# Three PSUM banks for side work: handed out by name from a list of free ones, in place of strictly in turn

## The chip, the cores and the metric

The kernel runs on one core of a Trainium2 chip. The metric is the device time of one execution in microseconds (us), lower is better. The engines are TensorE (PE; its weight loads are a row of their own, PEld), VectorE (DVE), ScalarE (ACT), GpSimd (POOL) and SyncE (SP, which here only issues DMAs).

## The reference, cut to what matters

Sixteen sequences of 512 tokens and 256 channels go through two layers, each followed by a residual sum and a layer norm. All arithmetic is in float32.

```python
# layer 1: a state-space layer, run forward and backward in time, 512 inner channels, 16 states
xf = silu(causal_conv(x @ in_proj_w.T)); xb = silu(causal_conv(xf))
delta, B, C = split(x_dbl); delta = softplus(delta @ dt_proj_w.T + b)
xs = cumsum(dB_u * dA_cum, 1) / (dA_cum + 1e-12)          # per channel and state
y  = einsum('bldn,bln->bld', xs, C) + u * D; y = y * silu(res)
# layer 2: a soft mixture of 16 experts with 64 slots each
logits = x2 @ se; dispatch = softmax over tokens; combine = softmax over slots
slots = dispatch.T @ x2; eout = (gelu(slots @ Wg + bg) * (slots @ Wu + bu)) @ Wd + bd
out = combine @ eout
```

## The kernel before, in words

**The scan.** For each sequence b (16 of them, called batches here) there are four parts, (direction r, pair of 128-channel chunks p) in the order (0,0), (1,0), (0,1), (1,1). A part goes over the 16 states two at a time and, inside, over its two chunks, so a part has 16 steps and a batch has 64. A step has a fixed chain over the engines: POOL multiplies `db` (L427), ACT makes the decay `h` and the factor `th` (L444, L446), DVE scans and multiplies (`h` L450 or L452, `hg` L455), POOL multiplies `hg` by `cs` (L456), and PE adds `hg` into an accumulator by transposing it (`acc`, L371), two steps later (`add_up(2)`). The buffers are three `db`, four `hg`, three `th`, three `h` in PSUM and two accumulators in PSUM.

**Diagonal states.** For two of the sixteen states (`DIAG`, 5 and 13) the product `db` is not made on POOL but on PE, as four matmuls with a diagonal matrix into a PSUM bank (`hd`, L405, function `by_diagonal`). Such a bank is taken one step before the step that scans it, at steps 3, 4, 11 and 12 of a part, and is held until the scanning step has been written out, the next step. DVE then scans in that bank.

**Side work.** All else is written as Python generators that are stepped while the scan is written out, and so are woven into its instruction order: `prep` (projections, convolution and step sizes of the next part: `pin`, `px`, `pz`, `pdu`, `pres`, `pb`), `front` (the end of layer 1 and the dispatch for the previous batch: `pyt`, `po`, `px2`, `pl`, `pd`, `pq`) and `back` (experts for two batches, and the combination: `pg`, `pu`, `peo`, `cl`, `ctp`, `cpo`). `back` gets a group of two batches every second batch, so odd batches hold the experts and even ones most of the combination. A generator yields how many PSUM banks its next piece needs; after it has written a product into a bank it yields `HOLD`, and the instructions that read the bank are written out one step later (`take_up`). In each step `beside_scan` first takes up what is held and then offers each of the three sides one piece, `front` and `back` at a pace (`paced_piece`: a credit, never above 2). `front.drain()` writes out at the end of a batch what is left of `front`.

**The banks.** Of PSUM's eight banks the scan has five; side work and the diagonal products share three (`m_ps`). They are used strictly in turn: a counter of products taken, `count`, stands for the ring. A side may go on only if the ring would not come round to a bank that is still held:

```python
oldest = min([x.hold for x in sides if x.hold is not None] + diags[:1], default=count[0])
if count[0] - oldest + self.need > BANKS:
    break
```

After the scan (the tail: end of layer 1 for the last batch, its experts and combinations) the five others are added, and the ring has eight.

The instructions of each engine stay in the order in which they are written out, except for those that the framework's scheduler is free to move; the framework puts a wait in front of the first matmul of a product until the bank's last reader has finished.

Of the kernel before, what the change touches and what calls it, by code (L numbers as in the profile page):

```python
# [9 lines left out]
F32 = mybir.dt.float32  # L10
# [4 lines left out]
PSUM = bass.MemoryType.PSUM  # L15
DRAM = bass.MemoryType.DRAM

P = 128
# [21 lines left out]
HOLD, WAIT, GAP = -1, -2, 8  # L40
# [15 lines left out]
def seq_layers(tc, ident, neghalf, a, out):  # L56
# [22 lines left out]
    with ExitStack() as ctx:  # L79
# [11 lines left out]
        scan_room = ctx.enter_context(ExitStack())  # L91
        p4 = scan_room.enter_context(tc.tile_pool(name="m_scan", bufs=3))
        dram = ctx.enter_context(tc.tile_pool(name="m_dram", bufs=3, space=DRAM))
        ps = ctx.enter_context(tc.tile_pool(name="m_ps", bufs=3, space=PSUM))
        scan_psum = ctx.enter_context(ExitStack())
        ps_acc = scan_psum.enter_context(tc.tile_pool(name="m_acc", bufs=2, space=PSUM))
        ps_h = scan_psum.enter_context(tc.tile_pool(name="m_h", bufs=3, space=PSUM))
# [1 line left out]

        BANKS = 3
        AHEAD = 8
        tail, wide = [], []
        count = [0]

        def bank(name):
            count[0] += 1
            if tail and count[0] % 8 >= 3:
                return tail[0].tile([P, 512], F32, tag="tps", name=name)  # L110
            return ps.tile([P, 512], F32, tag="mps", name=name)

        def load_x(b):
            xt = p1.tile([P, NL, DM], F32, tag="x", name=f"x_{b}")
# [12 lines left out]
        def late(ins):  # L127

            return tc.keep_in_program_order(ins)
# [258 lines left out]
        def evict():  # L388
            while evictions:
                evictions.pop(0)()  # L390

        def scan_part(b, r, p, v, accs, done, then):

            prep.drain()
            prep.gens += [[1, g] for g in [turn_pair(b, r, p, v)] + then]
            w = side[r]
            made = {}

            def by_diagonal(n, c):

                diags.append(count[0])
                made[n, c] = h = bank(f"hd_{b}_{r}_{n}_{c}")
                for lc in range(NL):
                    s = slice(lc * P, (lc + 1) * P)
                    ins = nc.tensor.matmul(h[:, s], v[c][3][:, s], dg[:, s], start=True, stop=True)  # L405
                    if lc == 0:
                        late(ins)

            chunks = (2 * p, 2 * p + 1)
            for n in range(0, NS, 2):  # L410
                q = f"{b}_{r}_{p}_{n}"
                k = 1 if n + 1 in DIAG else 2

                bs = p4.tile([P, 2, L], F32, tag="bs", name=f"bs_{q}")
                cs = p4.tile([P, 2, L], F32, tag="cs", name=f"cs_{q}")
                nc.sync.dma_start(bs[:, :k, :], v["bc"][0, n : n + k, :].unsqueeze(0).to_broadcast([P, k, L]))
                nc.sync.dma_start(cs, v["bc"][1, n : n + 2, :].unsqueeze(0).to_broadcast([P, 2, L]))
                if n + 3 in DIAG:
                    dg = p4.tile([P, L], F32, tag="dg", name=f"dg_{q}", bufs=1)
                    nc.sync.dma_start(  # L420
                        dg.rearrange("p (l s) -> p l s", l=NL),
                        diag_dram[r, DIAG.index(n + 3), :, : P * P].rearrange("l (p s) -> p l s", p=P),
                    )
                for c in chunks:
                    dt, rr, du = v[c][:3]
                    db = p4.tile([P, 2, L], F32, tag="db", name=f"db_{q}_{c}")
                    nc.gpsimd.tensor_tensor(  # L427
                        db[:, :k, :], du.unsqueeze(1).to_broadcast([P, k, L]), bs[:, :k, :], ALU.mult
                    )
                    hg = p4.tile([P, 2, L], F32, tag="hg", name=f"hg_{q}_{c}", bufs=4)  # L430
                    hs = {}
                    for j in range(2):
                        if j < k:
                            dec = h = ps_h.tile([P, L], F32, tag="h", name=f"h_{q}_{c}_{j}")
                            hs[j] = (h, dec, db[:, j, :])
                        else:
                            h = made.pop((n + j, c))
                            dec = p4.tile([P, L], F32, tag="dec", name=f"dec_{q}_{c}", bufs=2)
                            hs[j] = (h, dec, h)

                    ths = {}
                    for j in range(2) if k == 2 else (1, 0):
                        s = slice(n + j, n + j + 1)
                        nc.scalar.activation(hs[j][1], dt, AF.Exp, scale=w["A"][:, c, s])  # L444
                        ths[j] = p4.tile([P, L], F32, tag="th", name=f"th_{q}_{c}_{j}")
                        nc.scalar.activation(ths[j], rr, AF.Tanh, bias=LN_1E12 / 2, scale=w["Ah"][:, c, s])  # L446
                    for j in range(2):
                        (h, dec, add), th = hs[j], ths[j]
                        if r == 0:
                            nc.vector.tensor_tensor_scan(h, dec, add, 0.0, ALU.mult, ALU.add)  # L450
                        else:
                            nc.vector.tensor_tensor_scan(  # L452
                                h[:, ::-1], dec[:, ::-1], add[:, ::-1], 0.0, ALU.mult, ALU.add
                            )
                        nc.vector.scalar_tensor_tensor(hg[:, j, :], th, 1.0, h, ALU.add, ALU.mult)  # L455
                    nc.gpsimd.tensor_tensor(hg, hg, cs, ALU.mult)  # L456
                    pending.append(
                        (r == n == 0, n == 0, r == 1 and n == NS - 2, c, hg, accs, w, v["u"], f"acc_{q}_{c}", done)
                    )
                    evict()  # L460

                    nxt_n = n if c == chunks[0] else n + 2
                    if nxt_n + 1 in DIAG:
                        for x in sides:
                            x.take_up()
                        by_diagonal(nxt_n + 1, chunks[1] if c == chunks[0] else chunks[0])
                    beside_scan()
                    if k == 1:
                        diags.pop(0)
                    add_up(2)  # L470

        class Side:


            def __init__(self):
                self.gens, self.hold, self.need, self.left, self.credit = [], None, 0, 0, 0.0
                self.wait = self.took = self.gap = False

            def add(self, steps, gen):
                self.gens.append([steps, gen])  # L480
# [3 lines left out]

            def go(self):

                at = count[0]
                mark = next(self.gens[0][1], None)
                self.wait = mark == WAIT
                if mark == HOLD:  # L490
                    self.hold = at if self.hold is None else self.hold
                    return
                self.hold, self.gap, self.need = None, False, 0
                if mark is None:
                    self.gens.pop(0)
                elif not self.wait:
                    self.gap, self.need = mark >= GAP, mark % GAP

            def take_up(self):
                self.took = self.hold is not None or self.wait  # L500
                if self.took:
                    self.go()

            def piece(self, gaps=True):

                done = False
                while self.gens and self.hold is None and not self.wait:
                    if self.gap and self.took and gaps:
                        break
                    oldest = min([x.hold for x in sides if x.hold is not None] + diags[:1], default=count[0])  # L510
                    if count[0] - oldest + self.need > BANKS:
                        break
                    done = True
                    head = self.gens[0]
                    head[0] = max(head[0] - 1, 1)
                    fresh = len(head) == 2
                    if fresh:
                        head.append(True)
                    self.go()
                    if not fresh and (not self.gens or self.gens[0] is head):  # L520
                        break
                return done
# [14 lines left out]
        diags = []  # L537
# [3 lines left out]
        def beside_scan():  # L541
            for x in sides:
                x.take_up()
            prep.piece()
            for x in (front, back) if front.credit > back.credit else (back, front):
                x.paced_piece(gaps=not hurry)
# [478 lines left out]
        add_up(0)  # L1025
        evict()
        scan_psum.close()
        tail.append(ctx.enter_context(tc.tile_pool(name="t_ps", bufs=5, space=PSUM)))
        scan_room.close()
        wide.append(ctx.enter_context(tc.tile_pool(name="t_sb", bufs=1)))  # L1030
        BANKS = 8

        def side_by_side():
            while front.gens or back.gens:
# [61 lines left out]
```

## Time and profile before

| | us |
|---|---|
| median of 3 runs (5407.39 to 5412.11) | 5410.29 |
| the profiled execution, its time | 5411.23 |
| its span, first to last instruction | 5409.4 |
| busiest engine over the span, POOL | 4732.1 |
| start of the first batch's scan to the end of the last one's | 48.8 to 5132.3 |
| one even batch in the middle, and one odd one | 308.3 and 326.6 |
| the last batch | 369.8 |
| the tail after the scan | 277.1 |

An engine's busy time is what its own rows sum to; a wait is idle time of the waiting engine, put down to what ended it last. Batch limits are the ends of POOL's `hg` of a batch's last step. PE's times are modelled and its matmuls overlap, so PE is read by its waits more than by its share. The mean granted clock of TensorE was 0.889.

### The profile page before, as it was taken

Reading aid. Unit: us, or ns where it says so; the run is one execution under the profiler, and the core shown is the slowest. Engines: PE = TensorE matmul, PEld = TensorE weight load, DVE = VectorE, ACT = ScalarE, POOL = GpSimd, SP = SyncE. Lnnn points to the kernel's source line nnn. Section 1 sums busy time; section 2 is a strip of 40 time slices with the busy share of each in tenths; the row PEclk is TensorE's granted clock in tenths of the full one; section 3 lists DMA queues with packets and bytes.
Section 4 is the critical chain, followed back from the end, with each engine's and each line's share of the span. In section 5 each row is a group of like instructions: output and inputs, shape, how many; then the busy total and the mean of one; then the engine's idle time right before and its main releaser. Section 6 shows DMA issues by size and latency. Waiting matters only on the chain. (4 is left out here: it accounts for less than half of the span.)

```text
span 5409.4 us, 73721 instructions
## 1 busy us (share of the span) xinstructions
PE 4331.1 (80%) x24144; PEld 3390.0 (63%) x24145; DVE 4559.7 (84%) x6276; ACT 4087.2 (76%) x6515; POOL 4732.1 (87%) x2537
## 2 busy tenths in 40 slices
PE   5656666898888978788888977889787897888889
PEld 3445555676666666677656765667656776667657
DVE  7888988889898899888998888988899889988722
ACT  6677777787888778887877887788788887877641
POOL 6999999999999899998999989998999989988600
PEclk7778778898899988899888989899889998989999
DMA  4334333575446644566446754467444764457436
GB/s 137 131 117 137 125 129 131 189 230 159 156 142 212 225 149 148 158 223 213 131 144 194 232 170 153 132 212 232 149 149 146 225 224 134 145 179 234 126 103 188
DMA packets 595236, 907.73 MB, mean 168 GB/s; under 512 B 78082, under 2 KB 384898, under 8 KB 594852
## 3 DMA queue, kind: packets, MB, share of 16 engines
q1 hardware_dynamic: 521156, 859.87, 49.5%
q10 hardware_dynamic: 73696, 43.14, 2.8%
q8 instruction: 192, 3.15, 0.2%
q14 instruction: 192, 1.57, 0.1%
HBM read 840.86 MB, written 62.01 MB: 167 GB/s over the span
## 5 line engine op out<-in xcount | busy, mean ns | idle before, releaser
L456 POOL TENSOR_TENSOR hg<-hg,cs 128x1024 f32<-128x1024 f32 x1024 | 2420.8, 2368 | 128.1 <-DVE hg L455 110.0
L427 POOL TENSOR_TENSOR db<-du,bs 128x1024 f32<-128x1024 f32 (+1 forms) x1024 | 2144.4, 2098 | 232.3 <-DVE h L450 84.7
L371 PE MATMUL acc<-ident,hg 128*128 128x128 f32 x8192 | 1179.3, 295 | 203.3 <-POOL hg L456 181.6
L455 DVE SCALAR_TENSOR_TENSOR hg<-th,h 128x512 f32<-128x512 f32 x1792 | 1185.8, 678 | 177.2 <-PE acc L371 90.4
L371 PEld LDWEIGHTS acc<-ident,hg 128*128 128x128 f32 x8192 | 1044.9, 154 | 390.8 <-POOL hg L456 240.9
L452 DVE TENSOR_TENSOR_SCAN h<-h,db 128x512 f32<-128x512 f32 x896 | 1072.8, 1218 | 112.2 <-ACT h L444 107.5
L450 DVE TENSOR_TENSOR_SCAN h<-h,db 128x512 f32<-128x512 f32 x896 | 1071.1, 1217 | 48.8 <-ACT h L444 45.7
L446 ACT ACTIVATE th<-rr,Ah_f 128x512 f32<-128x512 f32 x1024 | 725.0, 714 | 186.3 <-DVE hg L455 183.1
L446 ACT ACTIVATE th<-rr,Ah_b 128x512 f32<-128x512 f32 x1024 | 721.5, 712 | 155.2 <-DVE hg L455 147.7
L444 ACT ACTIVATE h<-dt,A_f 128x512 f32<-128x512 f32 x896 | 608.2, 680 | 117.5 <-DVE hg L455 112.6
L444 ACT ACTIVATE h<-dt,A_b 128x512 f32<-128x512 f32 x896 | 608.6, 681 | 108.8 <-DVE hg L455 105.1
L687 PE MATMUL pl<-x2T,seT 128*128 128x512 f32 x512 | 299.1, 715 | 78.7 <-DVE hg L455 37.4
L405 PE MATMUL hd<-dg,duT 128*128 128x128 f32 x2048 | 305.6, 298 | 32.7 <-ACT yt L627 13.5
L830 PEld LDWEIGHTS pg<-st,Wg 128*128 128x128 f32 x2048 | 244.8, 196 | 106.2 <-issue 85.0
L405 PEld LDWEIGHTS hd<-dg,duT 128*128 128x128 f32 x2048 | 283.1, 214 | 38.4 <-ACT yt L627 15.7
L806 PE MATMUL peo<-Wd,ht 128*128 128x256 f32 x1024 | 257.0, 407 | 55.6 <-DVE rr L337 38.6
L779 PE MATMUL pu<-st,Wu 128*128 128x128 f32 x2048 | 254.5, 283 | 50.1 <-DMA Wu<-in_Wu_dram 32.7
L962 PE MATMUL cpo<-ceo,ct 128*128 128x256 f32 x1024 | 254.8, 407 | 46.9 <-DVE rr L337 39.9
L779 PEld LDWEIGHTS pu<-st,Wu 128*128 128x128 f32 x2048 | 244.9, 198 | 61.5 <-DVE h L452 24.2
L830 PE MATMUL pg<-st,Wg 128*128 128x128 f32 x2048 | 269.9, 286 | 4.1 <-DMA Wg<-in_Wg_dram 3.1
L884 PE MATMUL cl<-seT,cx 128*128 128x512 f32 x512 | 244.7, 617 | 32.5 <-DVE res L272 12.3
L806 PEld LDWEIGHTS peo<-Wd,ht 128*128 128x128 f32 x1024 | 205.3, 206 | 97.7 <-DVE rr L337 41.2
(154 smaller groups left out, 6654.8 us busy)
## 6 DMA issues: line engine op xcount, KB each, us to landing
cs<-bc SPq DMA_DIRECT2D x512, 512.0 KB, 3.9
bs<-bc SPq DMA_DIRECT2D x384, 512.0 KB, 5.1
Wg<-in_Wg_dram SPq DMA_DIRECT2D x128, 512.0 KB, 6.0
Wu<-in_Wu_dram SPq DMA_DIRECT2D x128, 512.0 KB, 6.0
Wd<-in_Wd_dram SPq DMA_DIRECT2D x128, 512.0 KB, 5.5
dg<-diag_dram SPq DMA_DIRECT2D x128, 256.0 KB, 4.2
bs<-bc SPq DMA_DIRECT2D x128, 256.0 KB, 3.6
x<-in_x_dram SPq DMA_DIRECT2D x32, 512.0 KB, 6.3
```

The source lines that it names most:

```text
L371: ins = nc.tensor.matmul(accs[c][:, s], hc[:, j, s], ident, is_transpose=True, start=False, stop=(last and j == 1 and lc == NL - 1),)
L405: ins = nc.tensor.matmul(h[:, s], v[c][3][:, s], dg[:, s], start=True, stop=True)
L427: nc.gpsimd.tensor_tensor(db[:, :k, :], du.unsqueeze(1).to_broadcast([P, k, L]), bs[:, :k, :], ALU.mult)
L444: nc.scalar.activation(hs[j][1], dt, AF.Exp, scale=w["A"][:, c, s])
L446: nc.scalar.activation(ths[j], rr, AF.Tanh, bias=LN_1E12 / 2, scale=w["Ah"][:, c, s])
L450: nc.vector.tensor_tensor_scan(h, dec, add, 0.0, ALU.mult, ALU.add)
L452: nc.vector.tensor_tensor_scan(h[:, ::-1], dec[:, ::-1], add[:, ::-1], 0.0, ALU.mult, ALU.add)
L455: nc.vector.scalar_tensor_tensor(hg[:, j, :], th, 1.0, h, ALU.add, ALU.mult)
L456: nc.gpsimd.tensor_tensor(hg, hg, cs, ALU.mult)
L779: nc.tensor.matmul(pu[:, fc * P : (fc + 1) * P], got["Wu", e][:, k, fc * P : (fc + 1) * P], st[:, k, :, j * SL : (j + 1) * SL], start=(k = ...
L806: nc.tensor.matmul(po[:, j * DM : (j + 1) * DM], ht[:, fc, :], got["Wd", e0 + j][:, fc, :], start=(fc == 0), stop=(fc == NF - 1),)
L830: nc.tensor.matmul(pg[:, fc * P : (fc + 1) * P], got["Wg", e][:, k, fc * P : (fc + 1) * P], st[:, k, :, j * SL : (j + 1) * SL], start=Fals ...
```

## The change

Banks now have names: each of the three is a pool tag of its own with one buffer, `mps0` to `mps2`. A list `free` holds the banks that nobody holds, in the order in which they were given back. `bank()` takes the first of the list and notes it in `taken`; a side keeps its own in `held` and gives them back when the instructions that read them have been written out; a diagonal product keeps its one in `diags` until its scanning step is over. A side may go on if as many banks are free as its next piece needs. Where a diagonal product is to be made and no bank is free, the one of the diagonal product just scanned is taken. In the tail the list has eight banks.

```diff
-        ps = ctx.enter_context(tc.tile_pool(name="m_ps", bufs=3, space=PSUM))
+        ps = ctx.enter_context(tc.tile_pool(name="m_ps", bufs=1, space=PSUM))
...
-        BANKS = 3
...
-        count = [0]
+        free, taken = [0, 1, 2], []
         def bank(name):
-            count[0] += 1
-            if tail and count[0] % 8 >= 3:
-                return tail[0].tile([P, 512], F32, tag="tps", name=name)
-            return ps.tile([P, 512], F32, tag="mps", name=name)
+            i = free.pop(0)
+            taken.append(i)
+            pool = ps if i < 3 else tail[0]
+            return pool.tile([P, 512], F32, tag=f"mps{i}", name=name, bufs=1)
...
-                diags.append(count[0])
                 made[n, c] = h = bank(f"hd_{b}_{r}_{n}_{c}")
+                diags.append(taken.pop())
...
+                    own = [diags.pop(0)] if k == 1 else []
                     if nxt_n + 1 in DIAG:
                         for x in sides:
                             x.take_up()
+                        if not free:
+                            free.append(own.pop())
                         by_diagonal(nxt_n + 1, chunks[1] if c == chunks[0] else chunks[0])
                     beside_scan()
-                    if k == 1:
-                        diags.pop(0)
+                    free.extend(own)
                     add_up(2)
...
             def go(self):
-                at = count[0]
                 mark = next(self.gens[0][1], None)
-                self.wait = mark == WAIT
-                if mark == HOLD:
-                    self.hold = at if self.hold is None else self.hold
+                self.held += taken
+                taken.clear()
+                self.hold, self.wait = mark == HOLD, mark == WAIT
+                if self.hold:
                     return
-                self.hold, self.gap, self.need = None, False, 0
+                free.extend(self.held)
+                self.held, self.gap, self.need = [], False, 0
...
-                    oldest = min([x.hold for x in sides if x.hold is not None] + diags[:1], default=count[0])
-                    if count[0] - oldest + self.need > BANKS:
+                    if self.need > len(free):
                         break
...
-        tail.append(ctx.enter_context(tc.tile_pool(name="t_ps", bufs=5, space=PSUM)))
+        tail.append(ctx.enter_context(tc.tile_pool(name="t_ps", bufs=1, space=PSUM)))
...
-        BANKS = 8
+        free.extend(range(3, 8))
```

More of the change, by code (lines that the diff above doesn't have):

```diff
@@ L475, in __init__ @@
             def __init__(self):
-                self.gens, self.hold, self.need, self.left, self.credit = [], None, 0, 0, 0.0
-                self.wait = self.took = self.gap = False
+                self.gens, self.held, self.need, self.left, self.credit = [], [], 0, 0, 0.0
+                self.hold = self.wait = self.took = self.gap = False
             def add(self, steps, gen):
@@ L499, in take_up @@
             def take_up(self):
-                self.took = self.hold is not None or self.wait
+                self.took = self.hold or self.wait
                 if self.took:
@@ L506, in piece @@
                 done = False
-                while self.gens and self.hold is None and not self.wait:
+                while self.gens and not self.hold and not self.wait:
                     if self.gap and self.took and gaps:
                         break
-                    oldest = min([x.hold for x in sides if x.hold is not None] + diags[:1], default=count[0])
-                    if count[0] - oldest + self.need > BANKS:
+                    if self.need > len(free):
                         break
```

## The prediction, made before the changed kernel was run

> **What bounds the kernel now.** I read the shares of the page first, then busy times by batch, then POOL's waits, then what stands behind them. In the page, look at POOL's share and at its row of the slices.
>
> ```profile
> PE 4331.1 (80%) x24144; PEld 3390.0 (63%) x24145; DVE 4559.7 (84%) x6276; ACT 4087.2 (76%) x6515; POOL 4732.1 (87%) x2537
> ...
> POOL 6999999999999899998999989998999989988600
> ```
>
> POOL is at nine tenths or more until the scan is over. The stage table says how near to its limit each batch is: an even batch, an odd one, the last, and the tail.
>
> ```profile
> core 0: us, PE busy (x) PEld busy (x) DVE busy (x) ACT busy (x) POOL busy (x), PEclk, DMA share, GB/s
> 1911.80:2220.10 308.30, 244.40 (x1274) 185.14 (x1272) 282.27 (x385) 247.85 (x414) 295.22 (x158) 0.87 0.44 140
> 2220.10:2546.70 326.60, 283.57 (x1747) 230.77 (x1746) 284.01 (x397) 261.99 (x399) 295.28 (x157) 0.94 0.66 214
> ...
> 4762.50:5132.30 369.80, 313.56 (x1835) 251.42 (x1834) 284.74 (x416) 265.33 (x416) 288.00 (x152) 0.92 0.58 188
> 5132.30:5409.40 277.10, 248.38 (x1248) 184.74 (x1246) 67.52 (x191) 77.30 (x153) 14.68 (x44) 0.97 0.46 142
> ```
>
> POOL is busy for 295 us in both kinds of batch, and the change gives it nothing less to do. So a scan batch can lose only what POOL sits idle: 13 us of an even batch, 31 of an odd one, 82 of the last. The tail is bound by PE, 248 of 277 us. POOL's waits inside the scan name DVE first:
>
> ```profile
> POOL hg L456 <- DVE hg L455: 110.0, 57, 6.3
> POOL db L427 <- DVE h L450: 84.7, 52, 6.6
> ...
> POOL db L427 <- DVE h L452: 57.2, 34, 6.3
> ```
>
> All of POOL's waits there sum to 358 us. One step further back, DVE waits for PE where a banked product or an accumulator is late:
>
> ```profile
> DVE hg L455 <- PE acc L371: 90.4, 82, 4.8
> DVE hd L452 <- PE hd L405: 76.4, 50, 8.0
> ```
>
> With `hd` on L450 (30.0) that is 197 us. And PE itself waits for banks. These four rows are waits for the last reader of a bank's former product: `rr` (L337) reads `pz`, and `hg` on L455 reads a diagonal bank.
>
> ```profile
> PE cpo L962 <- DVE rr L337: 39.9, 10, 6.4
> PE peo L806 <- DVE rr L337: 38.6, 12, 6.6
> PE pl L687 <- DVE hg L455: 37.4, 12, 5.0
> ...
> PE px L668 <- DVE hg L455: 31.7, 6, 6.1
> ```
>
> Following each product's bank to its last reader, such waits come to 579 us of PE, 345 of them at the four steps of a part in which a diagonal bank is taken (steps 3, 4, 11 and 12: 60 + 78 + 71 + 135). The timeline shows one reach POOL, at the ninth step of an even batch:
>
> ```profile
> 1959.93 1.98 PE L405 MATMUL hd<-dg,duT 128*128 128x128 f32 x8 [2.25 <-ACT yt L627]
> ...
> 1962.01 1.23 DVE L450 TENSOR_TENSOR_SCAN hd<-dec,hd 128x512 f32<-128x512 f32 x1 [2.48 <-PE hd L405]
> ...
> 1966.42 2.35 POOL L427 TENSOR_TENSOR db<-du,bs 128x1024 f32<-128x1024 f32 x1 [1.51 <-issue]
> ```
>
> The diagonal product waited 2.25 us for a bank that ACT was to copy out, DVE's scan 2.48 us for the product, and POOL lost 1.51 us. But most do not arrive: even batches have 48 us of PE bank waits each and 13 us of idle POOL, odd ones 34 and 31.
>
> **What the Trainium skill says.** "PSUM — Partial Sum Buffer", section "Engine vs sequencer instructions": matmuls start and complete in program order. The trace agrees: where `pd` waited 3.31 us for a diagonal bank at 2485.92 us, the accumulation behind it began only after it. The same page's summary tells to guard PSUM by bank; here every product does wait for its bank's last reader. "Perfetto Trace Analysis", section "Optimization Strategy": a gap that repeats on the engine that should be full can mean too little PSUM for the next tile. The gaps do repeat (`px` six times, once per even batch), though on PE and not on POOL. "ScalarE: Activation LUTs", section "What ACT_TABLE_LOAD costs", gives 1283 ns for a load; the trace has 1283 ns.
>
> **The change part by part.** Matmuls, reads, DMAs and POOL's instructions are the same in number; only places and banks change.
>
> *Side work moves forward.* In the order written out, `cl`, `ctp`, `cpo` stand 5.5, 5.0 and 4.8 steps earlier on average, `pg`, `pu`, `peo` 3.1, `pl` 1.2, `pd` 1.5; `hd` and `pdu` stay. Twelve pieces that `front.drain()` wrote at batch ends (one `pq` in each of twelve batches) go into the scan. POOL's idle time there is near zero at the last three steps, so this is worth nothing by itself; the scan's next steps are its cover, and without it 12 x 3.5 us = 42 us would be at stake.
>
> *What moves along.* A piece's DMAs go with it on SP: an expert's `Wg`, `Wu`, `Wd` (0.4 us to issue, 6.0, 6.0, 5.5 to landing) pass some `bs` and `cs` loads. These are asked for up to three buffers ahead, about 15 us at 5 us a step against 5.1 and 3.9 to landing, and that hides it; with the cover gone, POOL's 69 us of `db` waits with no releaser shown ("issue") would be where it shows, by 0.4 us for each load passed, at most 19 us for an odd batch's 48. On POOL the layer norms' small operations move too (four of 0.2 to 1.0 us per norm), same count, 0.
>
> *Between batches.* Moving forward takes work out of even batches and into odd ones. Pricing each product by its PE time in the chain (32 `pu` or 8 `cl` records 3.5 us, others by their columns), that is 7.8 us of PE from each even batch to an odd one. From the table, 39 us more PE goes with 18 us more POOL idle, 0.47 per us, so +3.7 us in six odd batches and as much less in six even: 0.
>
> *Tail.* One `cl` pair fewer is left over: 8 records of the 3.45 us that the chain shows for such a group, on the engine that sets the tail: -3.5 us.
>
> *Table loads.* ACT has 334 loads for 337; the last batch has 25 for 32. 7 x 1.283 = 9 us of ACT there, in the batch with 82 us of idle POOL. ACT waits for DVE and DVE for ACT in turn (`h` L452 for ACT `h` 107.5 us), so I let half through: -4.5 us.
>
> *Banks.* For each product I set how many steps its bank's last reader stands ahead of the last accumulator step before it. With DVE as reader, four steps ahead cost 2.2 us on average before and three steps 0.97; 54 and 285 products become 40 and 332. With ACT, four steps cost 0.62, and 296 become 342. All distances weighted so, PE's waits before products go from 806 to 818 us: no gain in the sum. They change place, though. Products that waited for a diagonal bank (about 104 us: the `pl`, `px` rows and `pd` 18.6, `pyt` 8.5, `cl` 7.5) mostly no longer do: the distance of four before such a bank occurs three times in two batches before and once after. The waits that take their place fall on other products, and odd batches lose the pair that stood straight before idle POOL (`pd` on the diagonal bank 3.3 us, then POOL 5.1; `pl` on `pz` 3.1, then POOL 2.6). Passed on at the whole kernel's ratio, 358 us of POOL wait to 806 of PE wait, 0.44, two thirds of 104 us are -31 us; the waits that come instead (+12 net over all, so +81 in places) I charge at 0.2, because they are shorter (means of 0.6 to 1.0 us, that the three `db` and four `hg` buffers hold off): +16 us. Bounds: nothing replaces them, -46 us at full rate; all pass at 0.44, +5 us.
>
> *Free-list test in place of the ring.* No instruction. A product that goes ahead where the ring had held it brings its reader into ACT or DVE one step later, ahead of the scan's own `th` or `hg` queued there; ACT's excess over POOL in stretches of four steps grows from 115 to 145 us (loads of each engine between scan steps, row means). At 0 to 1, 0 to +30 us; I take 0, since DVE's falls by 22.
>
> Sum: -3.5 - 4.5 - 31 + 16 = -23 us on the profiled execution's 5411.2 (0.9 above the median): 5388.
>
> **The rivals.** *A, the waits only move.* The weighted sum says so outright (806 to 818), and the even batches show PE waits that cost POOL nothing. Then only the tail's 3.5 us is left: 5407. Against it: two of an odd batch's largest POOL gaps follow bank waits that go. *B, slower: the diagonal product queues behind `pz`.* A pair of `pz` banks is given back with `rr` only just written into DVE's queue, and `by_diagonal` comes right behind. Diagonal products on a `pz` bank whose reader was written out at most one step earlier go from 17 to 47. `cpo` and `peo` waited up to 6.4 and 6.6 us in that seat. A late diagonal product stops DVE's scan, which nothing passes; 30 more at the sample's 1.51 us of POOL idle are +45 us, 5455. For it: the scan depends on `hd` directly and on `cpo` only through PE's order. Against it: most such readers stand two steps ahead, a distance that cost `hd` 0.2 us on average. It decides once PE's waits in front of `hd`, 33 us now, pass some 80. *C, it doesn't free the ring.* Where two sides hold two and one bank, nothing is free either way and the order stays; the moved positions above exclude that.
>
> **How the numbers follow.** A measurement of this kernel tells about 0.2%, 11 us, from no change. Faster as summed 0.50, A 0.20, B and other harmful places 0.30. The same pattern repeats in six pairs of batches, so 5 us per pair is already 30: the faster case's own range is 5335 to 5398. The range to B's end is 5335 to 5455, with one in ten outside on each side.
>
> **What would show it.** Right: POOL waits in the scan below 340 us, odd batches at 322 or less, even ones at 308 or less, tail about 274, `pl` and `px` no longer waiting for `hg` L455. A: the same waits under other names, batches within 1 us. B: DVE `hd` waiting for PE `hd` well over 106 us, odd batches above 330. Wrong altogether: POOL's busy time per batch changed, or a tail longer by more than 5 us.

## The result, and the profile after

The change makes the kernel slower: 5461.65 us median (5445.26 to 5467.65) against 5408.84 us for the kernel before on the same chip, ratio 1.0092, interval 1.0069 to 1.0116. The prediction was 5388 us with a range to 5455 us, so both the sign and the range missed. The profiled execution took 5445.26 us, the shortest of its runs; what is taken apart below is its 34 us over the profiled one of before. Where the 16 us up to the median lie, no trace shows.

The page of the changed kernel, shares and POOL's row of the 40 slices:

```profile
PE 4326.4 (79%) x24131; PEld 3376.8 (62%) x24145; DVE 4561.5 (84%) x6276; ACT 4082.7 (75%) x6512; POOL 4737.9 (87%) x2537
...
POOL 6999999998999899998999989999899989987810
```

No engine has noticeably more to do than before (POOL 4737.9 us for 4732.1); POOL's row only goes on one slice longer. The stage table of the changed kernel, for an even batch, an odd one, the last, and the tail:

```profile
core 0: us, PE busy (x) PEld busy (x) DVE busy (x) ACT busy (x) POOL busy (x), PEclk, DMA share, GB/s
1935.20:2245.50 310.30, 240.87 (x1291) 180.97 (x1290) 282.91 (x384) 248.78 (x414) 295.26 (x157) 0.92 0.44 137
2245.50:2580.10 334.60, 288.61 (x1725) 232.49 (x1727) 283.77 (x398) 262.41 (x402) 295.83 (x157) 0.92 0.66 211
4824.50:5194.30 369.80, 309.03 (x1818) 248.61 (x1820) 282.49 (x413) 254.32 (x407) 288.11 (x151) 0.93 0.59 184
5194.30:5443.10 248.80, 236.14 (x1230) 176.90 (x1229) 66.84 (x190) 76.98 (x153) 14.79 (x45) 1.00 0.50 158
```

Two things happened. The scan ends at 5194.3 us instead of 5132.3, 62 us later, with POOL as busy per batch as before: the odd batch shown has 39 us of idle POOL for 31, the even one 15 for 13. And the tail is 28 us shorter, 248.8 for 277.1. The sum is the 34 us.

POOL's waits inside the changed kernel's scan (us in total, times, longest):

```profile
POOL db L427 <- issue: 114.8, 59, 3.6
POOL hg L456 <- DVE hg L455: 84.9, 64, 6.8
POOL db L427 <- DVE h L452: 84.6, 41, 6.1
POOL db L427 <- DVE h L450: 77.8, 67, 3.5
```

The same first row in before's view:

```profile
POOL db L427 <- issue: 69.2, 33, 3.2
```

All rows summed alike over each kernel's scan, POOL waits 422 us, before 366. The row that grew most is `db` "issue", 69 to 115 us; `db` behind DVE's `h` on L452 grew by 27 and `hg` fell by 25. "Issue" isn't a late load here: the `bs` loads are asked for over 20 us ahead and land after some 4 us, and all 59 of these waits end 0.13 us behind one of DVE's scans, which gives a `db` buffer back. Behind them stand DVE's own waits, same stretch:

```profile
DVE h L452 <- ACT h L444: 126.4, 82, 6.8
DVE hg L455 <- PE acc L371: 113.6, 81, 6.8
DVE hd L452 <- PE hd L405: 78.4, 42, 7.5
DVE h L450 <- ACT h L444: 57.3, 71, 5.9
...
DVE hd L450 <- PE hd L405: 19.9, 22, 4.5
```

Before's rows for ACT's decays, which the prediction did not show:

```profile
DVE h L452 <- ACT h L444: 107.5, 94, 6.2
...
DVE h L450 <- ACT h L444: 45.7, 33, 3.4
```

This is the reading that the prediction lacked: it followed DVE's waits back to PE alone. All rows in which DVE waits for ACT sum to 295 us, before 240; all in which it waits for PE to 300 us, before 314. So the added waits of DVE are booked to ACT, not to late banks. (A wait is booked to what ended it last; the third set of experiments comes back to this.) PE's own waits for the last reader of a bank, counted alike over both whole traces, are 643 us after and 642 before. They did change place; three of the new rows of PE:

```profile
PE pres L212 <- DVE res L272: 50.9, 9, 8.4
PE hd L405 <- DVE rr L337: 46.3, 16, 5.4
...
PE px L670 <- DVE res L272: 36.4, 6, 8.0
```

Most of the tail's gain, 20 of the 28 us, lies in one place, the dispatch of the last batch. The first table is of before, the second of the changed kernel; the second row of each is that stretch:

```profile
5132.30:5177.00 44.70, 40.70 (x190) 30.54 (x189) 12.60 (x35) 14.06 (x31) 3.28 (x8) 0.98 0.39 127
5177.00:5248.00 71.00, 57.97 (x202) 34.04 (x200) 16.20 (x42) 31.59 (x67) 1.70 (x4) 0.93 0.14 45
```

```profile
5194.30:5234.50 40.20, 37.07 (x178) 27.19 (x178) 12.50 (x34) 14.06 (x31) 3.33 (x9) 1.00 0.41 136
5234.50:5285.60 51.10, 50.52 (x204) 31.16 (x203) 15.01 (x41) 31.25 (x67) 1.70 (x4) 1.00 0.20 66
```

71.0 us became 51.1 for the same products, and PE, idle for 13 us there before, is busy throughout. PE's waits in that stretch, before and after:

```profile
PE pd L704 <- ACT et L700: 10.2, 4, 3.5
```

```profile
PE pd L706 <- ACT et L702: 0.6, 1, 0.6
```

These are not waits for banks. `pd` waits for its own input `et`, which ACT makes from `pl`. In before's trace PE takes `pd` straight behind `pl` four times, in the changed kernel's twice, since parts of `cl` and of the next `pl` stand between.

### The profile page after: what moved, and what is told of

Read it like the earlier page. It is cut to its first block, busy times and chain, and to the rows that moved or that the text cites. A ratio compares the mean times of both kernels' runs of the same rounds, so it can differ in the third digit from the quotient of the medians.

```text
span 5443.1 us, 73707 instructions
## 1 busy us (share of the span) xinstructions
PE 4326.4 (79%) x24131; PEld 3376.8 (62%) x24145; DVE 4561.5 (84%) x6276; ACT 4082.7 (75%) x6512; POOL 4737.9 (87%) x2537
## 5 line engine op out<-in xcount | busy, mean ns | idle before, releaser
L452 DVE TENSOR_TENSOR_SCAN h<-h,db 128x512 f32<-128x512 f32 x896 | 1077.3, 1222 | 130.7 <-ACT h L444 126.4
L444 ACT ACTIVATE h<-dt,A_f 128x512 f32<-128x512 f32 x896 | 611.1, 683 | 134.7 <-DVE hg L455 130.5
L444 ACT ACTIVATE h<-dt,A_b 128x512 f32<-128x512 f32 x896 | 608.7, 681 | 123.8 <-DVE hg L455 122.5
L405 PE MATMUL hd<-dg,duT 128*128 128x128 f32 x2048 | 315.0, 303 | 104.9 <-DVE rr L337 46.3
L689 PE MATMUL pl<-x2T,seT 128*128 128x512 f32 x512 | 286.5, 685 | 86.1 <-ACT cm L900 19.3
L964 PE MATMUL cpo<-ceo,ct 128*128 128x256 f32 x1024 | 237.4, 386 | 31.9 <-DVE rr L337 14.1
L721 PE MATMUL pq<-dis,xn 128*128 128x256 f32 x1024 | 244.8, 393 | 15.2 <-ACT cm L900 15.2
```

The lines of the kernel that those rows point to most:

```text
L452: nc.vector.tensor_tensor_scan(h[:, ::-1], dec[:, ::-1], add[:, ::-1], 0.0, ALU.mult, ALU.add)
```

## The experiments

One point of the text ahead is wrong. It says that before's three banks are used strictly in turn. Its `count` assumes that; but a tag with three buffers hands out whichever buffer the framework finds free as it places the instructions, and in the program as built only about 45 in 100 products take the next bank in turn. So the change has three parts, not two: the **test** (ring or free list), the **choice of bank in the scan** (the framework's, or the list's by name), and the choice **in the tail**. The table collects every kernel by these parts; "held" and "diagonals" mean the ring test against these banks alone. Times are us; the ratio is to before on the same chip and comes from all executions of a kernel, while a scan end and a tail are read from its one profiled execution. Executions of one kernel lie up to 30 us apart (e11; after 22, e1 16), so a difference of 10 or 20 us between two scan ends is read together with the medians.

| kernel | test | choice in scan / tail | scan end | tail | ratio, interval |
|---|---|---|---|---|---|
| before | ring | framework / framework | 5132.3 | 277.1 | 1 |
| e4 | ring | framework / framework | 5132.7 | 281.8 | 0.9997, 0.9989 to 1.0005 |
| e5 | ring | framework / names | 5132.4 | 257.5 | 0.9964, 0.9952 to 0.9976 |
| e1 | ring | names / names | 5158.4 | 250.4 | 0.9983, 0.9977 to 0.9990 |
| e2 | ring | names in turn / same | 5263.2 | 252.2 | 1.0169, 1.0151 to 1.0187 |
| after | free list | names / names | 5194.3 | 248.8 | 1.0092, 1.0069 to 1.0116 |
| e3 | free list | framework / framework | 5214.2 | 274.6 | 1.0133, 1.0119 to 1.0148 |
| e6 | ring: diagonals | names / names | 5180.2 | 251.2 | 1.0042, 1.0029 to 1.0055 |
| e7 | ring: held | names / names | 5275.8 | 251.8 | 1.0207, 1.0193 to 1.0221 |
| e17 | ring: `prep` only | names / names | 5227.6 | 246.5 | 1.0126, 1.0108 to 1.0145 |
| e18 | ring: `prep` only | framework / names | 5182.9 | 250.7 | 1.0068, 1.0048 to 1.0089 |

In the diffs below, lines that only keep the old count are left out.

**First set: the parts one by one.** e1 keeps the changed kernel's names and lets the old test decide, so that side work is written out exactly as before:

```diff
-                    if self.need > len(free):
+                    oldest = min([x.at for x in sides if x.at is not None] + marks[:1], default=count[0])
+                    if count[0] - oldest + self.need > BANKS:
```

> Side work stands at exactly the steps of the kernel before (its ring test decides when a side may go on); only the bank of each product comes from the list of free names, as in the changed kernel. Theory N (fixing a bank by name at the time of writing costs, because the pool no longer gives a product whichever buffer comes free): slower than before by 25 us or more, 5435 to 5465, tail near 277. Theory G (side work going ahead past held banks is what costs): as before, 5400 to 5415.

e2 is before with its banks named strictly in turn, the tail's five likewise:

```diff
-            return ps.tile([P, 512], F32, tag="mps", name=name)
+            turn[0] += 1
+            return ps.tile([P, 512], F32, tag=f"mps{turn[0] % 3}", name=name, bufs=1)
```

> The kernel before with its three banks named and taken strictly in turn (and the five of the tail likewise); steps of side work as before. In the kernel before the two shared buffers were not in strict turn: of its products only some 45 in 100 took the next bank. Theory N: slower than before, 5430 to 5490, since a held diagonal bank is now really waited for. Theory G: as before, 5400 to 5420.

e3 has the changed kernel's test, with one tag of three buffers (five in the tail) again:

```diff
-            return pool.tile([P, 512], F32, tag=f"mps{i}", name=name, bufs=1)
+            return pool.tile([P, 512], F32, tag="mps" if i < 3 else "tps", name=name)
```

> The changed kernel's test (enough banks free) and so its steps of side work, but banks from one pool tag with three buffers (five more in the tail), so that the pool chooses as in the kernel before. Theory N: as before or faster, 5380 to 5415. Theory G: as the changed kernel, 5440 to 5470.

e4 is before with `back` shifted against `front` at the start of the tail's first `side_by_side()`:

```diff
+        back.take_up()
+        back.piece()
```

> The kernel before, with one piece of the back side written out ahead at the start of the tail, so that the combination stands one round earlier against the dispatch, as it does in the changed kernel. The changed kernel's tail took 248.7 us, before 277.1; of that 20 us lie in the dispatch of the last batch. If the phase of the two sides is what did it: 5385 to 5395. If the named banks did it: 5405 to 5412.

Against what was expected: e1's median, 5407.69 us, lies where theory G put it, but only because 26 us more of scan and 27 us less of tail cancel. e2 (5513.26 us) and e3 (5488.61) came out slower than either theory allowed. e4 (5415.74) excludes the phase of the two sides and lies 4 us above the range for named banks.

What follows, by scan ends. With names, the new test costs 36 us (e1 to after); with the framework's choice it costs 82 us (before to e3). Names cost 26 us in the scan under the old test (before to e1) and gain 20 under the new one (e3 to after). Strictly in turn would have cost 131 us, which shows that before does not do it. In the tail, names give about 25 us (before to e1, e3 to after) whatever the test, and strictly in turn (e2) as well; the shift of `back` against `front` isn't the reason (e4). e3's tail, new test without names, is 2.5 us shorter than before's.

A name does more than pick a bank: the framework then places the instructions in another order, though they are written out alike. Of ACT's 6178 instructions other than table loads, 5223 stand at the same place in the traces of before and e1. In the tail this is what can be seen to pay: PE's waits there sum to 22 to 23 us in the three kernels without names (before, e3, e4) and to 3 to 8 us in e1, e2, e5 and after. In the scan, order and bank change together in e1, and no run here parts them.

**Second set: names in the tail only, and the test in halves.** e5 has before's scan and names only for the tail's five banks (against e1):

```diff
             i = free.pop(0)
             taken.append(i)
-            pool = ps if i < 3 else tail[0]
-            return pool.tile([P, 512], F32, tag=f"mps{i}", name=name, bufs=1)
+            if i < 3:
+                return ps.tile([P, 512], F32, tag="mps", name=name)
+            return tail[0].tile([P, 512], F32, tag=f"mps{i}", name=name, bufs=1)
```

> The scan is that of before: ring test, one tag of three buffers, the framework's own choice of bank. Only the five banks added for the tail have names and are taken from the free list. Theory (naming shortens the tail by itself, whatever the scan does): the scan ends where before's did, near 5132 us, the tail is near 250 us, the median near 5385 us, 0.995 of before. Rival (the tail is shorter only because the scan ahead of it ended differently): the tail stays at 275 us or more and the median at 5409 us.

Measured: 5392.63 us against 5413.33, scan end 5132.4, tail 257.5. The tail's gain is its own, 8 us short of what I expected. This kernel beats before and after: its order in the scan is before's (6166 of ACT's 6178 instructions at the same place).

e6 and e7 split the 213 places where the old test stops a side and the new one doesn't: e6 keeps the ring for diagonal banks (149 places), e7 for held banks (64).

```diff
-                    oldest = min([x.at for x in sides if x.at is not None] + marks[:1], default=count[0])
-                    if count[0] - oldest + self.need > BANKS:
+                    oldest = min(marks[:1], default=count[0])
+                    if self.need > len(free) or count[0] - oldest + self.need > BANKS:
```

e7 has the other half of the minimum:

```diff
+                    oldest = min([x.at for x in sides if x.at is not None], default=count[0])
```

> Banks named from the free list as in after; a side goes on only if enough banks are free and, besides, the old ring would not come round to the bank of a diagonal product still in use. Products that two-step holds of another side would have stopped (64 of the 213 places that differ) go ahead; the 149 that a diagonal bank would have stopped do not. Theory D (going ahead past a diagonal bank is what costs): scan end near that of the old test with the free list, 5158 to 5166 us, median 5408 to 5418 us. Rival H (going ahead past the held banks costs): scan end near 5194 us, median near 5445 us. Rival S (both cost in proportion to their number): scan end near 5169 us, median near 5419 us.

> The other half: enough free banks and, besides, the ring test against the banks that sides hold, without the diagonal ones; so the 149 places of the diagonal banks go ahead and the 64 others do not. Theory D: scan end 5186 to 5200 us, median 5437 to 5462 us. Rival H: scan end near 5160 us, median near 5410 us. Rival S: scan end near 5183 us, median near 5434 us.

Measured: 5433.22 and 5524.77 us; scan ends 22 and 117 us behind e1's, where the whole new test is 36 behind. e6 lies between S and H, e7 outside all three: this half of the test costs three times the whole. The cost isn't a sum over the places that go ahead; it depends on what meets what afterwards. One thing more can be counted in the kernels as written: e6 leaves every product of preparation at before's step, and only `front` and `back` go ahead; e7 moves preparation exactly as after does, and `back` less far (`pg` 2.6 steps for 3.1, `cl` 3.9 for 5.5).

**Third set: does the cost come through ACT?** In the traces a load of ACT's function table (`ACT_TABLE_LOAD`, 1.28 us) stands in front of Softplus, Silu or Gelu where they follow the scan's Exp and Tanh, and another where the scan goes on; with all three replaced by Exp and Tanh, one load is left in the whole trace. In the changed kernel's trace one can see such loads meet side work. In a window of batch 1, where little side work runs beside the scan, ACT loads Softplus's table at 626.69 us straight behind side work, without a decay (`h`, L444) of the scan between:

```profile
625.95 0.72 ACT L702 ACTIVATE et<-et,sm 128x512 f32<-128x512 f32 x1 [0.92 <-DVE sm L701]
626.69 1.28 ACT L320 ACT_TABLE_LOAD   x1
...
627.98 0.60 ACT L320 ACTIVATE dt<-pz 128x512 f32<-128x512 f32 x1
628.48 0.59 ACT L324 ACTIVATE dt<-pz 128x512 f32<-128x512 f32 x1
...
629.08 1.28 ACT L444 ACT_TABLE_LOAD   x1
630.38 0.69 ACT L444 ACTIVATE h<-dt,A_b 128x512 f32<-128x512 f32 x1
...
631.17 1.23 DVE L452 TENSOR_TENSOR_SCAN h<-h,db 128x512 f32<-128x512 f32 x1 [4.09 <-ACT h L444]
...
634.51 1.27 POOL L427 TENSOR_TENSOR db<-du,bs 128x512 f32<-128x512 f32 x1 [0.77 <-DVE h L452]
...
639.76 2.36 POOL L427 TENSOR_TENSOR db<-du,bs 128x1024 f32<-128x1024 f32 x1 [1.66 <-issue]
```

DVE's scan waits 4.09 us for the decay and POOL loses 0.77 and 1.66 us. With the old test (e1; its lines are 3 to 4 higher) the pair of Softplus comes one step later, after decays that keep DVE fed; DVE waits 2.77 us and POOL 0.83:

```profile
623.06 0.71 ACT L450 ACTIVATE th<-rr,Ah_b 128x512 f32<-128x512 f32 x1
...
623.79 1.28 ACT L323 ACT_TABLE_LOAD   x1
...
628.75 1.23 DVE L456 TENSOR_TENSOR_SCAN h<-h,db 128x512 f32<-128x512 f32 x1 [2.77 <-ACT h L448]
...
632.94 2.36 POOL L431 TENSOR_TENSOR db<-du,bs 128x1024 f32<-128x1024 f32 x1 [0.83 <-POOL du L342]
```

To test it, functions are replaced so that all but one of ACT's table loads go, in after, in e1 and once in before. The number of other instructions, the names and the tests stay. The order doesn't quite: the framework places instructions anew, and of ACT's 6178 only 4229 stand at the same place in after and in after without loads (5331 without Gelu, 5740 without Silu, 5205 without Softplus):

```diff
-                    late(nc.scalar.activation(xf, xf, AF.Silu))
+                    late(nc.scalar.activation(xf, xf, AF.Tanh))
...
-                    act = nc.scalar.activation(dt, pz, AF.Softplus)
+                    act = nc.scalar.activation(dt, pz, AF.Exp)
...
-                    args = (ht.rearrange("p f s -> p (f s)"), pg, AF.Gelu)
+                    args = (ht.rearrange("p f s -> p (f s)"), pg, AF.Tanh)
```

> After, with Silu and Gelu replaced by Tanh and Softplus by Exp, so that nearly all of ACT's 334 function table loads (1.283 us each, 429 us) go; the values computed are others. All matmuls, banks, tests and the number of ACT's instructions stay. Theory T (going ahead costs through ACT: bunched evictions and table loads leave the scan's decays late): with ACT lighter by a tenth of its time the costs of the arrangement go: this kernel's scan ends at most 15 us later than that of before without table loads, against 62 us with them, while PE's waits for banks stay near 640 us. Rival P (it costs through PE's waits for banks): PE's waits stay and so does the difference, 45 us or more. Either way the scan can't be shorter than POOL's busy time, 4716 us.

> The old test with banks from the free list, with the same replacement of functions. Theory T: scan end within 10 us of after's without table loads (36 us earlier with them). Rival P: 25 us or more earlier.

> Before with the same replacement of functions: the yardstick of the two others. Its scan falls towards POOL's busy time in either theory; I expect its end between 4800 and 4950 us.

Then one function at a time, after and e1 each:

> After with Gelu alone replaced by Tanh, so that the experts' table loads go and those of Silu and Softplus stay; the values of the experts are others. Theory G (the loads that the new test bunches are the experts': an odd batch's last part has three Gelu loads beside two others between 2519 and 2531 us): this kernel's scan ends at most 15 us later than that of the old test with the same replacement, against 36 us with Gelu. Rival (any load matters where it falls): 25 us or more later.

> The old test with banks from the free list, with Gelu alone replaced by Tanh: the yardstick for the run before. I expect its scan to end between 5085 and 5125 us, 35 to 75 us earlier than with Gelu.

> After with Silu alone replaced by Tanh (other values of xf and xb). Theory L (the lump of Silu, 4.5 us of ACT with its two loads, meets others with the new test): scan end at most 15 us later than that of the old test with the same replacement. Theory K (the Softplus pairs): 25 us or more later. Rival sum (it is the total of the loads, whichever): about 25 us later, the 36 us less a share.

> The old test with banks from the free list, with Silu alone replaced by Tanh: yardstick of the run before. I expect its scan to end between 5135 and 5155 us.

> After with Softplus alone replaced by Exp (other values of dt). Theory L: scan end 25 us or more later than that of the old test with the same replacement. Theory K: at most 15 us later. Rival sum: about 20 us later.

> The old test with banks from the free list, with Softplus alone replaced by Exp: yardstick of the run before. I expect its scan to end between 5110 and 5145 us.

Scan ends, and DVE's summed waits for ACT in the scan:

| functions replaced | old test, names | new test, names | new test costs | by medians of time | loads, old / new | DVE for ACT, old / new |
|---|---|---|---|---|---|---|
| none | 5158.4 | 5194.3 | +36 | +59 | 321 / 334 | 264 / 295 |
| Gelu | 5117.5 | 5153.8 | +36 | +29 | 192 / 192 | 223 / 312 |
| Silu | 5126.9 | 5172.4 | +46 | +41 | 265 / 277 | 253 / 264 |
| Softplus | 5137.1 | 5121.9 | -15 | -17 | 205 / 214 | 295 / 279 |
| all three | 5065.3 | 5042.8 | -22 | -12 | 1 / 1 | 229 / 210 |

(The first median is worked out from the two ratios, since after and e1 ran on different occasions.)

As times: without loads after is at 5306.52 us and before at 5318.99, ratios 0.9816 (0.9802 to 0.9830) and 0.9827 (0.9814 to 0.9840) to the unaltered before. The scan of after then ends 6 us behind that of before (5042.8, 5036.8) instead of 62, while PE's waits for banks are alike in the two (538 and 534 us, less than the 640 that I expected). So without loads the test's cost is gone, as theory T said. That it turns into a gain is not clear of noise there: by medians it is 12 us, and the two ratios' intervals overlap (e9: 0.9829, 0.9815 to 0.9842). Where the loads go with Softplus alone, the gain is clear: every execution of e15 (5375.72 us at most) is faster than every one of e16 (5387.98 at least). T's forecast for e9, within 10 us of after's, missed: 22 us later. The Gelu theory and the Silu theory fell.

The number of loads isn't it. The new test has 13 more of them than the old, 17 us of ACT, but without Gelu the two have equally many and the cost stays, and without Softplus the new test has 9 more and gains. What these runs don't exclude is that the changed order, and not the loads themselves, takes part of the cost away. DVE's wait for ACT has the sign of the cost in all five pairs; it doesn't give the size. In the Gelu pair it rises by 89 us while DVE's wait for PE falls by 70 (330 to 260): what ends a wait last changes. Over all twenty kernels of this document the scan end follows the sum of DVE's waits for ACT and PE (correlation 0.97) more closely than those for ACT alone (0.85). Two yardsticks missed: before without loads (4800 to 4950 us expected, 5036.8 measured) and e14 (8 us earlier than expected).

**Fourth set: is it preparation's pairs one step early?** With the new test all but 2 of 32 `px` and 92 of 128 `pz` stand one step earlier. e17 leaves `prep` under the ring, so that they stand where before has them, and lets `front` and `back` alone go ahead; e18 does so with before's choice in the scan and e5's tail.

```diff
-                    if count[0] - oldest + self.need > BANKS:
+                    if self.need > len(free) or self is prep and count[0] - oldest + self.need > BANKS:
```

> Named banks from the free list; preparation keeps the ring test, so that all its products (px, pz, pin, pres, pb) stand at the steps of before; the other two sides go on if enough banks are free (pg 3.7, cl 5.7, pl 2.0 steps ahead on average). Theory K (preparation one step early is the cost): scan end 5165 us or earlier, median 5418 us or less. Rival F (the other sides' going ahead costs): scan end 5185 us or later, median 5436 us or more.

> The same tests, with the framework's choice among three buffers in the scan and named banks only for the tail's five. Theory K: scan end near before's 5132 us or earlier, median 5395 us or less, level with or faster than the names in the tail alone (5393 us). Rival F: scan end 5190 us or later, median 5440 us or more.

Measured: 5480.71 and 5445.62 us, scan ends 69 us behind e1's and 51 behind before's. K fell as the whole cause: e17 lies where rival F put it, e18 just short of F by its scan end and within F by its median. K holds where hardly anything but preparation runs: batches 1 and 2 take 301.8 and 301.9 us in e17, 301.1 and 301.9 in e1, 304.1 and 304.4 in after. From batch 3 on, the sides that go ahead cost more. e6 says the same: with preparation unmoved, `front` and `back` going less far ahead than in e17 (`pg` 2.6 steps for 3.7) cost 22 us. Taken with e15, this suggests that the test's cost needs Softplus's loads, but not that they stand one step early; e17 without Softplus's loads was not run. e17 shows the heaviest meeting of all; ACT and DVE of e17, an odd batch:

```profile
2344.02 1.28 ACT L860 ACT_TABLE_LOAD   x1
2345.36 0.60 ACT L860 ACTIVATE ht<-pg 128x512 f32<-128x512 f32 x1
2345.86 0.50 ACT L672 ACTIVATE xn<-x,m_r 128x256 f32<-128x256 f32 x1
2348.59 0.60 ACT L863 ACTIVATE ht<-pg 128x512 f32<-128x512 f32 x1 [2.23 <-PE pg L843]
2349.08 0.50 ACT L672 ACTIVATE xn<-x,m_r 128x256 f32<-128x256 f32 x1
2349.60 1.28 ACT L448 ACT_TABLE_LOAD   x1
2350.90 0.69 ACT L448 ACTIVATE h<-dt,A_b 128x512 f32<-128x512 f32 x1
...
2351.69 1.23 DVE L456 TENSOR_TENSOR_SCAN h<-h,db 128x512 f32<-128x512 f32 x1 [9.06 <-ACT h L448]
...
2355.83 2.37 POOL L431 TENSOR_TENSOR db<-du,bs 128x1024 f32<-128x1024 f32 x1 [9.99 <-DVE h L456]
```

An expert's two Gelu and pieces of a layer norm's scaling fall between the same two decays. ACT takes them as they stand, and even sits idle for 2.23 us until the second `pg` is there, with a piece of `xn` and the decay queued after it; that piece's inputs were ready since 2343.56 us. DVE waits 9.06 us and POOL 9.99. At this step POOL loses 9.3 us on average in the odd batches of e17, 3.2 in after, 3.5 in before. The Trainium skill, "Perfetto Trace Analysis", section "Tensor Engine Instruction (MATMUL, LD_WEIGHTS)", says that ACT, DVE and GPSIMD are strict FIFO; the 2.23 us with ready work behind agree. Here it is Gelu's load that stands in the way, not Softplus's.

## Why the prediction was wrong, point by point

*What bounds it.* POOL in the scan and PE in the tail: right. POOL's busy time per batch did not move. The reading behind it left things out: 358 us is the sum of the nine largest of POOL's rows, all make 366; and DVE's waits were followed to PE alone (197 us in three rows), though those for ACT make 240.

*Side work moves forward, DMAs, POOL's small operations: 0.* POOL's instructions cost nothing, as said, and the `bs` loads have more cover than the 15 us that I gave (over 20). But that forward move is not a part apart from the test; it is what the test does, and it is where the cost sits.

*Free-list test: taken 0 of 0 to +30.* **This is the step that failed.** With names the test measured +36 us in the scan, with the framework's choice +82, each net of all else that the test moves. I had the mechanism (a reader enters ACT's queue ahead of the scan's own work) and even its size (ACT's excess in four steps up by 30 us), and then struck it out against DVE's fall of 22. The two didn't offset: from e1 to after DVE's waits for ACT rose by 31 us and those for PE fell by 3. That the bound of 30 comes near 36 is in part luck, since the same test cost 82 with the framework's choice. At a price of one, the upper bound, the forecast would have been "no change".

*Banks: -31 + 16, from a sum that rises by 12.* That the sum hardly moves was right (642 to 643 us). The net gain of 15 us is not seen in the kernel as it is. With all table loads out the new test gains 22 us (12 by medians), with Softplus out 15; that a gain of this size from the banks lies under ACT's cost is an inference, since these runs lighten ACT too. That `pl` and `px` no longer wait for `hg` came true; `px` waits for `res` instead (36.4 us for 31.7), as rival A said of waits in general.

*Choice of bank.* This is the second thing that the sum lacked. The prediction had no term for it, because I took before to go strictly in turn. Under the old test names cost 26 us of scan. With all loads out they still do, 28 us (e10 to e9), so this part does not come from the loads; by medians, tails included, e9 and e10 are level (5318.94 and 5318.99 us), as e1 and before nearly are. What it comes from, the banks or the changed order, stays open: DVE's waits for PE fall by 10 us from before to e1 and rise by 27 from e10 to e9.

*Tail: -3.5.* Measured -28.3. The `cl` pair gave 2.5 (e3), close to the term; the rest is the names, which the prediction didn't price in the tail at all: with them PE's order there lets it wait less (22 us before, 6 after).

*Table loads: -4.5 from the last batch.* Its loads fell as counted (32 to 25), and it takes 369.8 us as before: 0 in all. Whether seven loads fewer gained something that the rest of the change took back, these runs don't show.

*Between batches: 0.* Odd batches rose by 5 us on average (5, 7, 9, 11, 13), but even ones from 4 on didn't fall, they rose by 3, and the first four by 20 together.

*Rival B.* PE's waits in front of `hd` went from 32.7 to 104.9 us, past the 80 that I gave as its point, but names under the old test bring them to 89.4 already (e1). Four of the five odd batches from 5 to 13 passed 330 us, where one had been before. But DVE's waits for `hd`, which were to show it, fell from 106 to 98 us. B gave nearly the right time (5455 us) for another reason, by luck. *C* is excluded by the order, *A* by the scan.

## What to carry to other kernels

A test that lets side work start as soon as a buffer is free also decides which engine's queue it lands in, and when; price it on the in-order engine that feeds the bound one, here ACT with its table loads, and do not offset that with slack on another engine of the same chain. Try such a test whole and in halves before trusting a sum over its places: here one half cost three times the whole. Before naming buffers, find out who chooses them now, stage by stage: under the old test the names are worth 20 us in the tail alone (e5, 5392.63 us, faster than before and after) and cost 26 in the scan. Compare the order of instructions in the two traces as well: a name alone can change it.

## What the hardware showed that I had not expected

Taking nearly all of 337 loads of 1.283 us, 432 us of ACT, out of before shortens its scan by only 95 us (e10), 0.22 per us. From the end of `et` at 626.67 us to the first Softplus at 627.98 us the switch cost 1.31 us in all, and the 315 switches of after's trace with no other wait around them took 1.30 to 1.43 us; the Trainium skill, "ScalarE: Activation LUTs", section "What ACT_TABLE_LOAD costs", adds a drain of about 1380 ns to the load, which this trace doesn't show. And in the tail's dispatch the granted clock was 0.93 with PE idle for 13 of 71 us, and 1.00 with PE busy throughout; the same products then took 50.5 us of busy PE for 58.0.
